# Four edits to a two-layer graph kernel: a sort moved by some products, banks of another pool, products with the identity, and joins a step later

## The chip, the cores and the metric

The kernel runs on one NeuronCore of a Trainium2 chip. The core has a matrix engine (TensorE, PE in the profile; PEld is its weight load), VectorE (DVE), ScalarE (ACT), GpSimd (POOL), and queues that start transfers (SP is SyncE's). Each engine works through its own instructions in their order and waits for others by semaphores. Matrix products go to PSUM, which has eight banks; a bank holds 128 rows of 512 float32 numbers.

The metric is the device time of one launch in microseconds (us). All times below are us unless they are marked otherwise.

## What is computed

`x` is 2708 x 1024 and `adj` 2708 x 2708, nearly all zeros and ones by a random draw whose density falls with the product of the row's and the column's weight: some rows have many neighbours, most only a few. Two layers follow each other, each with a residual and a layer norm:

```python
q, k, v = x @ W_q.T + b_q, x @ W_k.T + b_k, x @ W_v.T + b_v
z = scale * (q @ k.T) * adj
attn = softmax(where(z == 0, -10000, z), axis=1)
x = layernorm(x + relu(attn @ v))            # layer 0
x = layernorm(x + adj @ (x @ weight) + bias) # layer 1
```

## The kernel before

The kernel does not form the full score matrix. It lists each row's neighbours, gathers their rows of `x`, and does softmax and weighted sum over those alone. A second, dense way (`dense_part`) stands behind a flag and isn't taken for these inputs.

Rows are worked in 22 blocks of 128, after a sort by degree: block 0 holds the rows of highest degree, and the rows of the very highest ("the hub") are shared out over all partitions. `SLOTS` says how many neighbours a row of each block may have.

The stages, in the order of time:

1. *Weights and M.* W_q and W_k are transposed, and M = W_q^T W_k is formed in 28 steps (`product_of_m`), each of four matmuls of 128 x 128 by 128 x 512 into one bank; the profile shows two records for each float32 matmul, so 8 records a step. The steps follow Strassen's scheme with seven half products per pair of blocks. The partial sums of four accumulators `pa` are added to M by VectorE or copied by ScalarE (L322, L806) between the steps that reuse the same bank. Meanwhile VectorE lists the neighbours of the blocks of `adj` (`list_columns`: six FIND_INDEX8 at L237 and some small work for each block) and ScalarE counts them (`count_columns`, L253, 2.5 each). A block of `adj` lies in one of three buffers; when it is counted, `load_adj` issues the next load on SyncE's queue. `EARLY` blocks are listed during M, in even steps of its 28 products; the rest during the next stage.
2. *Four pairs of y blocks* (`y_pair`, blocks 0 to 7): y = x M by seven half products of 8 records per pair. VectorE adds three of the results (L322, yo), the others are copied by ScalarE; a pair's seventh product accumulates into a bank that one of these additions has to read first. `between` hangs pieces of other work behind the half products of this stage, by their running number (`began`): behind the first, third and fifth product of a pair a count, behind the second and fourth a list.
3. *Fourteen single y blocks* (`y_block`, and `y_last` for the rest of 20 rows), two banks of eight matmuls each; ScalarE copies the banks (L320). Beside them runs the attention of the high-degree blocks: GpSimd gathers rows (L464, L480), VectorE forms scores (L1016) and weighted sums (L1073, L1150), ScalarE exponentials (L1052, L1143). Which blocks are worked on beside which step follows from a planner with costs and a credit (`run_job`, `credit`).
4. *Ten pairs of blocks of layer 0* (`project_pair`), with their transposes (`flip`, L935), and one step for rows without neighbours ("mean").
5. *Layer 1*: ten units of two blocks, whose neighbours' normed rows are gathered from DRAM and summed (`sum_rows`, L1446, L1449), transposed and multiplied with the weight.

The sort has two halves, called families (blocks 0 to 7, and the rest). `sort_begin` makes class numbers from the degrees and one-hot rows `hot` on VectorE (L654 to L669), as soon as the family's blocks are listed and counted; `sort_end` multiplies them with a triangle and with ones on TensorE (L675, L679), turns the result into positions on VectorE (L683 to L690) and builds records. `records_out` scatters the records to DRAM by GpSimd (L704), eight instructions for the first family, then reads the tables back (L714 to L720). `deal_hub` is a generator whose parts are taken one at a time: it gathers the hub's records (L464, `rec_r`) and computes from them where the hub's rows lie (L533, `hub_i`).

In the version before, the first family's `sort_end` is called within M, after product 26, and its records go out behind the start of the first y pair's second product.

The hub and block 0 end with two "joins", in which the partitions that share a row agree on the maximum (transpose at L1158, VectorE at L1160 to L1165) and on the sum (matmul at L1168, VectorE at L1170 to L1173). `join(i, least)` runs a join at step `i` if the last part of this block was at least `least` steps ago.

PSUM is split into a pool of four banks for products (`bank()`, tile `po`), three banks for transposes (`spare_bank()` and tile `tr`) and one for small results (`mm`). Each pool hands its banks out in turn, and whoever is given a bank waits until its last reader is done.

The program is written in Python; the order of the instructions on each engine is made from it by the tile framework, which moves an instruction ahead of others that aren't ready by its own estimate. Additions and copies out of PSUM in `add` have high priority (`URGENT`). `follow(later, earlier)` adds a dependency by hand; with `same=True` it only fixes the order on one engine.

Of the kernel before, what the change touches and what calls it, by code (L numbers as in the profile page):

```python
# [27 lines left out]
HUB_SLOTS = 11  # L28
HUB_KEYS = 80
RUN = 12  # L30
FAMILY = 8


# [4 lines left out]
KEYS = 24  # L38
RANGES = 6
CLASSES = list(range(1, 14)) + [15, 17, 20, 24]  # L40
EARLY = 12
G1 = 9
RB = 5
REC = 28
# [38 lines left out]
def sparse_part(ctx, tc, x, xT, adj, wqT, wkT, wvT, bq, bk, bv, w1, b1, out):  # L83
# [28 lines left out]
    with es:  # L112
# [198 lines left out]
        def bank():  # L311
            return p_o.tile([P, HALF], F32, name="po")

        def spare_bank():
            return p_tr.tile([P, 4, P], F32, name="tr").rearrange("p a b -> p (a b)")
# [57 lines left out]
        def y_block(b):  # L373
            yo = yos[b % 3]
            to = halves_of(yo)
            firsts = []
            for h in range(NH):
                po = bank()
                for c in range(DC):
                    put = nc.tensor.matmul(po, xts[b][:, c, :], m_q[c // 4][h][:, c % 4], start=(c == 0), stop=(c == DC - 1))  # L380
                    if c % (DC // 2) == 0:
                        firsts.append(put)
                add(to[h], po, None)
            products.append(put)
            if b != NB - 2:
                column_sums(b, firsts)
            if b == NB - 4:
                column_sums(NB - 2, [put] * (DC // 2))
            load_x()
            y_store(b, yo)  # L390
# [280 lines left out]
        def sort_end(f, behind=None):  # L671
            b0, nb = families[f]
            bs, NKB = slice(b0, b0 + nb), NK * nb
            before = spare_bank() if f else p_mm.tile([P, HALF], F32, name="mm")
            put = nc.tensor.matmul(before[:, :NKB], lower, hot_f[f], start=True, stop=True)  # L675
            if behind is not None:
                follow(put, behind, same=True)
            total = spare_bank()
            nc.tensor.matmul(total[:, :NKB], ones, hot_f[f], start=True, stop=True)  # L679
            one_row = lists.tile([P, NKB], F32, name=f"one_row{f}")  # L680
            nc.vector.memset(one_row, 1.0)
            upto = lists.tile([P, NKB], F32, name=f"upto{f}")
            nc.vector.tensor_tensor_scan(upto, one_row, total[:, :NKB], 0.0, op0=ALU.mult, op1=ALU.add)  # L683
            nc.vector.tensor_sub(upto, upto, total[:, :NKB])
            nc.vector.tensor_add(upto, upto, before[:, :NKB])
            nc.vector.tensor_mul(upto, upto, hot_f[f])
            pos = lists.tile([P, nb], F32, name=f"pos{f}")
            nc.vector.tensor_reduce(pos, by_class(upto, nb).rearrange("p k b -> p b k"), AX.X, ALU.add)
            pos_i = (xa if f else lists).tile([P, nb], I32, name=f"pos_i{f}", bufs=1)
            nc.vector.tensor_copy(pos_i, pos)  # L690

            rec = (xa if f else lists).tile([P, nb, REC], I32, name=f"rec{f}", bufs=1)
            nc.vector.memset(rec[:, :, ROW:], 0)
            fill = lists.tile([P, nb, ROW], F32, name=f"fill{f}")
            nc.vector.tensor_scalar(fill, keys[:, bs, :], 0.0, float(N + 1), op0=ALU.is_equal, op1=ALU.mult)
            nc.vector.scalar_tensor_tensor(rec[:, :, 0:ROW], keys[:, bs, :], -1.0, fill, op0=ALU.add, op1=ALU.add)
            nc.vector.tensor_copy(rec[:, :, ROW], own[:, bs])
            nc.vector.tensor_copy(rec[:, :, DEG], deg[:, bs])
            nc.vector.tensor_scalar_add(rec[:, :, OFF], own[:, bs], float(-b0 * P))
            return f, nb, rec, pos_i  # L700
# [49 lines left out]
        def product_of_m(acc, a, w, start, stop):  # L750
            nonlocal done, worked
            put = half_products(acc, a, w, start, stop)
            worked += 1
            if counted[0] < done:
                count_columns(put)
            while done < EARLY * worked // (7 * DC // 2):
                list_columns()
                done += 1
                if done == FAMILY + 1:
                    sort_begin(0)  # L760
            if not sorted_ and done > FAMILY + 2 and worked > 7 * DC // 2 - 4:
                sorted_.append(sort_end(0, put))

        half = range(DC // 2)
        (w11, w12), (w21, w22) = wk_o
# [82 lines left out]
            count_columns(began[-1])  # L848
        for b in range(0, FAMILY, 2):
            first = len(began)  # L850
            for k in range(min(4 if b == 2 else 3, NB - done)):
                if k:
                    between[first + 2 * k] = [lambda put: list_columns()]
                else:
                    list_columns()
                done += 1
                between[first + 2 * k + 1] = [count_columns]
            if b == 4:
                between[first + 6] = [lambda put: next(deal)]
            if b == 6:  # L860
                between[first + 5] = [lambda put: next(deal)]
            y_pair(b)
            if b == 0:
                records_out(*sorted_[0], 0, FAMILY, began[first + 1])
                records_back(0)
            if b == 2:
                load_last()
                bcast_rows(y_bc, y_col)
            if b == 4:
                sort_begin(1)  # L870
            if b in (0, 6):
                next(deal)
            if b >= 4:
                load_wv(range(DC // 2 + b - 4, DC // 2 + b - 2))
# [469 lines left out]
        for i, (kind, b) in enumerate(steps):  # L1344
# [3 lines left out]
            pending = []  # L1348
            credit += COST.get(kind, COST.get(b, STEP - Y_END))
            step[0] = i  # L1350
            join(i, 2 if left_y else 1)
            if kind == "y" and b == NB - 3:
                (q11, q12), (q21, q22) = wv_q
                follow(nc.vector.tensor_sub(q12, q12, q11), products[-2])
# [124 lines left out]
        def work1(unit, A, S, xrs):  # L1479

            ts = [wa.tile([P, D], F32, name="t", tag="t" if k % 2 == 0 else "yg") for k, _ in enumerate(unit)]
            sums = [[stat.tile([P, 1], F32, name=f"sm{h}", bufs=6) for h in range(NH)] for _ in unit]

            def whole(k, h, acc, what):
                with tc.high_priority(URGENT):
                    nc.vector.scalar_tensor_tensor(halves_of(ts[k])[h], acc, 1.0, what, op0=ALU.mult, op1=ALU.add,  # L1486
                                                   accum_out=sums[k][h])
                    if k and unit == units[-1]:
                        if len(sums[k]) == NH:
                            sums[k].append(half_stats())  # L1490
                        nc.vector.bn_stats(out=sums[k][-1][:, h, :], in_=halves_of(ts[k])[h])

            xs_ = [halves_of(xr) for xr in xrs]
            pair_products(A, S, w1_q, w1_t, xs_, xs_, whole, unit == units[-1])
            return ts, sums

        got1, turned1, pending = {}, {}, []
        got1[0] = [sum_rows(b, k) for k, b in enumerate(units[0])]
# [349 lines left out]
```

## Time and profile before

| | |
|---|---|
| median of five runs | 1090.85 |
| lowest and highest of the runs | 1086.36 and 1091.83 |
| the profiled execution's own time | 1079.33 |
| its span | 1077.6 |
| busy: PE, DVE, POOL, ACT | 960.5, 839.8, 542.9, 411.0 |
| mean granted TensorE clock | 0.96 |

The stages as they stand in the profile, with what the windows of 20 us give for TensorE and VectorE:

| stage | about | PE busy of 20 | DVE busy of 20 |
|---|---|---|---|
| M's products | 28 to 137 | 20 up to 100, then 15.8 and 13.0 | 19.8 to 20.0 |
| pairs of y | 137 to 248 | 13.9 to 20 | 12.8 to 20 |
| single y blocks | 250 to 465 | 18 to 20 up to 340, then 10.1 to 19.7 | 7 to 18.5 |
| pairs of layer 0 | 472 to 769 | 14.9 to 20 | 13.4 to 20 |
| layer 1 | 777 to 1078 | 16.5 to 20 | 5.7 to 18.9 |

All profile numbers come from one execution, recorded by the hardware. In a timeline a line begins with the start and the duration in us, then engine, line of the kernel, operation, output and inputs, shape and the number of records; in brackets stands how long the engine was idle before and what ended that. In a list of waits the numbers are the total, how often, and the longest.

### The profile page before, as it was taken

How to read it: one execution, taken by the hardware profiler on the slowest of the kernel's cores; microseconds unless marked ns; L12 is line 12 of the kernel's file. 1: busy time of each engine (PE TensorE's matmuls, PEld its weight loads, DVE VectorE, ACT ScalarE, POOL GpSimd, SP SyncE). 2: the span in 40 equal slices, each digit the busy share in tenths (PEclk: the TensorE clock that was granted, in tenths of full speed). 3: DMA queues.
4: the chain of work that ended last, by engine and by line, in shares of the span. 5: the costliest groups of instructions: out<-in, count | busy, mean ns of one | idle time of the engine just before them, and what ended most of it. 6: DMA issues, size and time to landing. Idle time of an engine off the chain costs nothing.

```text
span 1077.6 us, 10401 instructions
## 1 busy us (share of the span) xinstructions
PE 960.5 (89%) x2697; PEld 451.0 (42%) x2697; DVE 839.8 (78%) x2033; ACT 411.0 (38%) x917; POOL 542.9 (50%) x447
## 2 busy tenths in 40 slices
PE   7999598999999796778999979999499999989894
PEld 6444233444444342334454434443154444445341
DVE  7999997974667777975999979777469878779532
ACT  4353175544532232422544444331312443351621
POOL 0431343122755655461767653346388877778510
PEclk9999799899999898889999999999789999999998
DMA  8565587388887665473558876479698789997731
GB/s 347 185 193 169 168 262 244 121 279 199 225 254 248 211 192 171 128 219 85 159 152 252 224 206 194 168 245 303 220 247 282 235 258 308 323 263 208 207 112 42
DMA packets 103069, 229.23 MB, mean 213 GB/s; under 512 B 19678, under 2 KB 47078, under 8 KB 103000
## 3 DMA queue, kind: packets, MB, share of 16 engines
q0 software_dynamic: 51152, 159.06, 49.1%
q1 hardware_dynamic: 51848, 69.41, 19.9%
q8 instruction: 23, 0.38, 0.1%
q14 instruction: 46, 0.38, 0.1%
HBM read 218.10 MB, written 33.64 MB: 234 GB/s over the span
## 4 chain that ended last, share of the span: by engine, by line
issue 17%; PE 15%; DMA 13%; DVE 12%; POOL 11%; ACT 1%; POOLq 0%; DVEq 0%; ACTq 0%
PE po L300 13%; POOL g L480 4%; DMA g<-in_x_dram,tabs 4%; DVE junkv L1016 3%; DMA g<-x_d,tabs 2%; POOL xr L464 2%; DMA xr<-x_d,tabs 2%; DVE r L1073 2%; DVE r L1449 1%; POOL g L464 1%; DMA yg<-y_d,tabs 1%; POOL tab_d L704 1%; DVE t L322 1%; DMA g<-in_x_dram,tab_h 1%; DMA g<-in_x_dram,tab 1%
## 5 line engine op out<-in xcount | busy, mean ns | idle before, releaser
L380 PE MATMUL po<-m,xt 128*128 128x512 f32 x416 | 187.1, 610 | 18.3 <-ACT yo L320 18.3
L300 PE MATMUL po<-t,s_all 128*128 128x512 f32 x320 | 148.3, 607 | 16.0 <-DVE t L322 8.0
L480 POOL DMA_INDIRECT g<-in_x_dram,tabs x84 | 113.3, 1349 | 87.2 <-issue 16.1
L380 PEld LDWEIGHTS po<-m,xt 128*128 128x128 f32 x416 | 80.9, 196 | 122.0 <-issue 98.8
L1016 DVE SCALAR_TENSOR_TENSOR junkv<-yg,g 128x1024 uint8<-128x1024 f32 x69 | 84.3, 1221 | 35.0 <-DMA g<-in_x_dram,tabs 24.3
L1449 DVE SCALAR_TENSOR_TENSOR r<-g,valid,r 128x1024 f32<-128x1024 f32 x77 | 98.3, 1282 | 12.9 <-DMA g<-x_d,tabs 12.5
L300 PEld LDWEIGHTS po<-t,s_all 128*128 128x128 f32 x320 | 61.1, 194 | 98.4 <-issue 70.8
L480 POOL DMA_INDIRECT g<-x_d,tabs x66 | 75.8, 1149 | 22.4 <-issue 15.9
L978 ACT ACTIVATE junks<-t,lnm 128x1024 uint8<-128x1024 f32 (+1 forms) x40 | 45.9, 1148 | 102.3 <-DVE lnm L976 99.8
L1073 DVE SCALAR_TENSOR_TENSOR r<-g,pr,r 128x1024 f32<-128x1024 f32 x64 | 81.8, 1280 | 4.0 <-ACT r L1071 3.7
L237 DVE FIND_INDEX8 at_a<-ones,a 128x8 uint16<-128x83 f32 (+3 forms) x132 | 82.8, 632 | 0.0
L300 PE MATMUL po<-wv,s_all 128*128 128x512 f32 x160 | 74.0, 606 | 7.4 <-DVE t L322 5.8
L253 ACT ACTIVATE junk<-a 128x2756 uint8<-128x2756 uint32 (+1 forms) x22 | 55.1, 2503 | 59.3 <-issue 22.1
L300 PE MATMUL po<-w,rT 128*128 128x512 f32 x160 | 73.8, 602 | 1.7 <-DVE t L1486 1.6
L300 PE MATMUL po<-t,rT 128*128 128x512 f32 x160 | 72.6, 595 | 1.7 <-DVE t L322 1.1
L300 PE MATMUL po<-wv,rT 128*128 128x512 f32 x160 | 72.7, 606 | 0.0
L300 PE MATMUL po<-w,s_all 128*128 128x512 f32 x160 | 72.3, 592 | 0.0
L936 ACT COPY rT<-tr 128x512 f32<-128x512 f32 x76 | 41.4, 586 | 74.7 <-PE tr L935 69.8
L991 ACT ACTIVATE t<-t,nmr,rstd 128x1024 f32<-128x1024 f32 (+1 forms) x40 | 49.1, 1240 | 53.4 <-DVE nmr L990 44.7
L453 ACT ACTIVATE junka<-xt 128x128 f32<-128x128 f32 x168 | 51.9, 309 | 36.5 <-PE po L300 25.9
L1016 DVE SCALAR_TENSOR_TENSOR junkv<-xr,g 128x1024 uint8<-128x1024 f32 x37 | 45.2, 1222 | 24.5 <-DMA g<-in_x_dram,tabs 11.2
L935 PE MATMUL tr<-ident,r 128*128 128x128 f32 x304 | 40.7, 283 | 23.4 <-DVE r L1446 14.3
(410 smaller groups left out, 1705.1 us busy)
## 6 DMA issues: line engine op xcount, KB each, us to landing
xt<-in_xT_dram SPq DMA_DIRECT2D x21, 512.0 KB
y_d<-yo SPq DMA_DIRECT2D x21, 512.0 KB
a<-in_adj_dram SPq DMA_DIRECT2D x21, 413.5 KB
a<-in_adj_dram SPq DMA_DIRECT2D x21, 338.5 KB
a<-in_adj_dram SPq DMA_DIRECT2D x21, 263.5 KB
wq_i<-in_wqT_dram SPq DMA_DIRECT2D x8, 512.0 KB
wk_i<-in_wkT_dram SPq DMA_DIRECT2D x8, 512.0 KB
wv<-in_wvT_dram SPq DMA_DIRECT2D x16, 256.0 KB
```

Of the source, the lines that this page charges most:

```text
L237: nc.vector.max_index(at[:n, i], ones[:n, :8], a[:n, cuts[i] + 8 * i:cuts[i + 1] + 8 * i + 8])
L253: put = nc.scalar.activation(junk[:n], loaded[b][:n, :AW].bitcast(U32), AF.Sign, accum_out=cnt[:n, b:b + 1])
L300: put = nc.tensor.matmul(acc, a[:, k], w[:, k], start=start and k == 0, stop=stop and k == DC // 2 - 1, skip_group_check=True)
L380: put = nc.tensor.matmul(po, xts[b][:, c, :], m_q[c // 4][h][:, c % 4], start=(c == 0), stop=(c == DC - 1))
L453: put = nc.scalar.activation(junka[:, :xt.shape[2]], xt[:, c, :], AF.Copy, accum_out=xs[:, c, b:b + 1])
L480: nc.gpsimd.indirect_dma_start(out=dst[:n], out_offset=None, in_=src, in_offset=bass.IndirectOffsetOnAxis(ap=at, axis=0), bounds_check=N - ...
L936: nc.scalar.copy(rT[:, g * 4:g * 4 + 4, :], tr)
L978: nc.scalar.activation(junks[:n], t[:n], AF.Square, bias=nm[:n], accum_out=vs[:n])
L991: applied.append(nc.scalar.activation(t[:n], t[:n], AF.Identity, bias=nmr[:n], scale=rstd[:n]))
L1016: nc.vector.scalar_tensor_tensor(junkv[:n], yg[:n], scale, xg[:n], op0=ALU.mult, op1=ALU.mult, accum_out=s)
L1073: nc.vector.scalar_tensor_tensor(r[:n], xg[j][:n], pr[:n, j:j + 1], r[:n], op0=ALU.mult, op1=ALU.add)
L1449: put = nc.vector.scalar_tensor_tensor(r[:n], xg[:n], ok[:n, j:j + 1], r[:n], op0=ALU.mult, op1=ALU.add)
```

## The change

Four edits are made at once:

- `EARLY` goes from 12 to 13, so one more block is listed during M, and the second y pair lists three blocks instead of four. The first family's `sort_end` is no longer called in `product_of_m`; it hangs behind the third half product of the first y pair, and the records go out behind the start of the fourth instead of the second.
- In `y_block`, blocks with a remainder of 1 by 3 (10, 13, 16 and 19) take their two banks from the transposes' pool instead of the products' pool.
- While y blocks are left, a join runs three steps after the last part of its block, not two.
- Between the layers TensorE gets 13 matmuls of the identity with half of `y_bc` (128 x 512, float32) into one bank of the transposes' pool. Nothing reads the result. They stand behind layer 0's last product in TensorE's order.

```diff
+WARM = 13
-EARLY = 12
+EARLY = 13
@@ y_block
-                po = bank()
+                po = spare_bank() if b % 3 == 1 else bank()
@@ product_of_m
-            if not sorted_ and done > FAMILY + 2 and worked > 7 * DC // 2 - 4:
-                sorted_.append(sort_end(0, put))
@@ the y pairs
-            for k in range(min(4 if b == 2 else 3, NB - done)):
+            for k in range(min(3, NB - done)):
...
+            if b == 0:
+                between[first + 3] = [lambda put: sorted_.append(sort_end(0, put))] + between.get(first + 3, [])
...
             if b == 0:
-                records_out(*sorted_[0], 0, FAMILY, began[first + 1])
+                records_out(*sorted_[0], 0, FAMILY, began[first + 3])
                 records_back(0)
@@ the steps of layer 0
-            join(i, 2 if left_y else 1)
+            join(i, 3 if left_y else 1)
@@ before layer 1's first sums
+        warm = spare_bank()
+        for k in range(WARM):
+            put = nc.tensor.matmul(warm, ident, y_bc[:, :HALF], start=True, stop=True, skip_group_check=True)
+            follow(put, products[-1], same=True)
```

## The prediction

> **What bounds the kernel now.** I read the table of windows first (which stage leaves which engine idle), then the waits of TensorE, then the timelines of the engines around each edit, then the chain that ended last.
>
> TensorE's waits, longest first: four of these rows are what the change aims at (ACT yo, DVE r L1446, DVE hot, DVE den).
>
> ```profile
> PE po L380 <- ACT yo L320: 18.3, 5, 9.9
> PE tr L935 <- DVE r L1446: 14.3, 1, 14.3
> PE mm L675 <- DVE hot L669: 11.2, 1, 11.2
> PE po L300 <- DVE yo L322: 10.3, 3, 6.1
> PE mm L1168 <- DVE den L1164: 5.0, 1, 5.0
> ```
>
> The first sort, TensorE's timeline: products 25 and 26 of M end at 115.8, the sort's matmul waits for its one-hot rows, products 27 and 28 follow in 8.94 where 16 such records take 7.03 elsewhere, and later two seventh products of y pairs wait for an addition.
>
> ```profile
> 108.78 7.03 PE L300 MATMUL po<-wk_o,wq_o 128*128 128x512 f32 x16
> 127.00 0.87 PE L675 MATMUL mm<-hot,lower 128*128 128x152 f32 x2 [11.19 <-DVE hot L669]
> 128.18 8.94 PE L300 MATMUL po<-wk_o,wq_o 128*128 128x512 f32 x16
> 136.96 7.03 PE L300 MATMUL po<-m,xt 128*128 128x512 f32 x16
> ...
> 160.32 3.70 PE L300 MATMUL po<-y_t,xt 128*128 128x512 f32 x8 [2.60 <-DVE yo L322]
> ...
> 190.77 6.72 PE L300 MATMUL po<-y_t,xt 128*128 128x512 f32 x8 [6.15 <-DVE yo L322]
> ```
>
> VectorE's side of it: from 40 to 160 the windows give it 19.8 to 20.0 busy of every 20, so it is the bound there and TensorE's waits are its symptoms. It adds M's last partial sum 14.7 after product 24 ended (108.8), and its only idle time before 190 is 7.20 for the hub's record.
>
> ```profile
> 123.47 0.68 DVE L322 TENSOR_TENSOR m<-po,m 128x512 f32<-128x512 f32 x1
> 159.59 0.68 DVE L322 TENSOR_TENSOR yo<-po,yo 128x512 f32<-128x512 f32 x1
> 167.46 0.21 DVE L533 TENSOR_SCALAR hub_i<-rec_r,g_col 128x1 int32<-128x1 int32 x1 [7.20 <-DMA rec_r<-tab_d,r_i]
> ```
>
> The single y blocks' end, ScalarE's timeline: the last two copies stand behind a softmax exponential that waits for VectorE, and the first transposes of layer 0's pairs are copied after them.
>
> ```profile
> 466.69 0.59 ACT L320 COPY yo<-po 128x512 f32<-128x512 f32 x1
> ...
> 469.94 0.29 ACT L1052 ACTIVATE pr<-scores,nms 128x2 f32<-128x2 f32 x1 [2.36 <-DVE nms L1043]
> ...
> 470.23 1.05 ACT L320 COPY yo<-po 128x512 f32<-128x512 f32 x2
> 471.18 1.57 ACT L936 COPY rT<-tr 128x512 f32<-128x512 f32 x3
> ```
>
> The change of layers: TensorE stands 14.31 and starts slow (8 transposes 1.94, later 1.04).
>
> ```profile
> 764.97 3.60 PE L300 MATMUL po<-t,rT 128*128 128x512 f32 x8
> 782.87 1.94 PE L935 MATMUL tr<-ident,r 128*128 128x128 f32 x8 [14.31 <-DVE r L1446]
> 784.63 2.07 PE L300 MATMUL po<-w,rT 128*128 128x512 f32 x2
> ```
>
> **Part 1, the first sort.** Removed: the wait of 11.19 in TensorE's queue. Moved: two matmuls (127.00 to 128.18, 1.2) behind the third product of the first y pair, VectorE's chain on them (133.05 to 135.27, 2.2), GpSimd's eight scatters of records (141.71 to 154.04) and, after them in its queue, the table reads and the hub's gather. Added to M's stage: one list of a block (4.70, the distance of the starts 77.10, 81.80, 86.50), taken from the second y pair (4 to 3). The counts behind the products come one or two products sooner, and with them their loads in SyncE's queue. These share it with the x tiles (issued at 107.58, landed at 116.08); the first sums of x are done at 126.0 and needed by the third y product, so some 5 us of delay there cost nothing.
>
> What is late next: product 28 accumulates into the bank that the addition at 123.47 reads, so without the sort TensorE still waits, from 119.2 (product 27 at 3.4) to 124.15. The first y product would start at 127.6 instead of 136.96, 9.4 earlier. By product 24 eleven lists are asked for instead of ten, so the addition moves by up to 4.7, and the gain shrinks to 4.7. Then the seventh y product: its addition ended at 160.27 with VectorE never idle since 40. With one list more ahead of it, it ends at 165.0, with none at 160.3; halfway, since the pair's own four lists fill that stretch either way: 162.6, so here TensorE is 2.3 later in spite of the wait removed. Then the hub's record. The scatters now follow the fourth product instead of the second. The sort's matmuls end at 132.3 + 10.3 + 1.2 = 143.8, VectorE's lag on them was 4.7 (128.4 to 133.05) and its chain 2.2, so the scatters start at 150.7 instead of 141.7, and the record lands at 176.5. If the instruction that needs it moves back in VectorE's order by as much, which two lists fill, the 7.20 vanish; the seventh product of the second pair is then limited by VectorE at 190.7 - 7.2 + 2.3 = 185.8 and by TensorE at 162.6 + 3.7 + 20.6 (163.86 to 184.5) + 1.9 for a slow start = 188.8. I take 188.8: 2 earlier, and a warm 3.6 instead of 6.72, together -5. From there every pair and the attention's first gathers (of stored y, at 255.57) follow TensorE, so it goes through. Ends: VectorE's limit without any more list, 183.5 (190.7 - 7.2), with the 3.1 of clock and the third pair's wait of 1.5: -12; and +8, worked out as the first rival. The value lies nearest to the limit by TensorE's own rows.
>
> **Part 2, banks of single y blocks, and the hub's joins.** Four blocks (10, 13, 16, 19) use two of the three transposes' banks; every block then needs the copy of three blocks ago instead of two, 13.8 us of room. The waits of 18.3 and, by the joins a step later, of 5.0 should go. But from 340 to 470 TensorE isn't on the chain: it goes through gathers, scores and sums (VectorE 13 to 18.5 of 20), and ScalarE's copies stand in its queue behind their exponentials. Block 20 ended at 464.9 and was copied at 470.23; were it done 20 earlier, the copy would still be behind the exponential at 469.94, and so the last store of y (471.31), the gather after it (478.98) and the transposes' copies. I cost both at 0: what hides them is that queue. If its order changes so that these copies come ahead of 465.62 (where ScalarE waits 4.40) they land up to 10 earlier: -10. Against it: block 19's banks are freed by the copy at 466.69, and the flips that started at 464.75 need them: +1.5 (three take 1.47). The bound stays near 0 as long as the copies stand where this row has them. [...]
>
> **Part 3, thirteen unit products.** One costs 0.86 (8 records, four products, every 3.43). 13 x 0.86 = 11.2 in an idle 14.31; 3.1 are left. The cold start costs 0.90 + 1.05 + 0.43 = 2.4 (8 transposes 1.94 against 1.04, 2 records 2.07 against 1.02, 8 transposes 1.47 against 1.04). Will 3.1 idle keep it warm? After 2.60 idle (160.32) 8 records took 3.70, after 3.06 (756.30) 5.40: so it may be cold again. And GpSimd issues gathers from 777.30 on with 0.30 between them, VectorE waits 1.14 for one at 824.57 and TensorE for VectorE at 834.99: most of what is won is gone by then. -1; ends -2.4 and +1.
>
> [...]
>
> **Sum:** -5 + 0 - 1 = -6 on the profiled execution's own 1079.33 us (span 1077.6): 1073.3. It lies 11.5 below the median of the runs (1090.85), so I carry the difference: 1085.
>
> **Rivals.** *The record comes too late (slower).* VectorE reaches the hub's instruction at 165.0 with one list more, in an unchanged order, and waits until 176.5: 11.5 instead of 7.20. The second pair's seventh product then comes at 190.7 + 9.0 (record) - 4.7 (list taken away) = 195, +4.3; the first pair's wait grows from 2.6 to 7 or more and costs a cold start on its path, some 3: +8 in all, 1099. It decides once VectorE's wait for the record exceeds 7.2 + 4.7 = 11.9 from its old place. For it: VectorE has no slack; against it: lists are there to fill the time. *The y pairs get all that VectorE allows:* -12, 1078. For it: additions are urgent in the order; against it: one list more. *ScalarE's order changes too:* -10 with the forecast's, 1075. Against it: nothing in part 2 makes the softmax earlier. *Nothing arrives:* part 1 at 0, 1090.
>
> **How the numbers follow.** Forecast 0.35 (own range 1081 to 1089), late record 0.25, VectorE's limit 0.12, ScalarE's order 0.12, nothing 0.16. A measurement of this kernel tells about 0.3% (3.3 us) from no change. Faster: 0.24 of the two early cases and 0.32 of the forecast, 0.56; same 0.19; slower 0.25. The range leaves out half of the tails beyond 1070 (both early cases together reach below it) and 1099.
>
> **What would show it.** Right: no wait on hot; a wait on m<-po's addition of about 5 to 10 before product 28; the seventh products of the first two pairs at about 163 and 189 from the span's start; hardly any wait of L380 but still copies at the attention's pace, ending some 5 before 470; 13 products behind 764, and nothing left of them at 835. Wrong: a wait at L533 above 12; last copies ahead of the last exponential; attention that starts later than 264.

## The result and the profile after

Over 44 runs the changed kernel took 1085.76 us in the median (1077.07 to 1094.01). 86 runs of the kernel before, on the same chips, took 1086.75 (1078.24 to 1095.54). The ratio is 0.999, with a 95% interval of 0.9977 to 1.0004: between 2.5 faster and 0.4 slower, and so no change that can be told. The forecast of 1085 lies beside it by luck, not by its own sum: it took 6 away from a median of five runs (1090.85) that was 4 too high.

The profiled executions differ by more than the kernels do: 1079.33 before, near the lower end of its runs, and 1086.25 after, about its median. What follows compares places within them, and lengths of stages, not their ends. Line numbers are one higher in every kernel that holds the unit products, L301 for L300.

TensorE's waits in the profile after, in the same view as before (total, how often, longest). The wait on the one-hot rows is gone, the five waits for copies of y (18.3) have become one of 25.0, ahead of the block of the last 20 rows, the wait for the first transposes' copies has grown from 5.6 to 17.2, and the 14.3 between the layers are 3.1:

```profile
PE po L432 <- ACT yo L321: 25.0, 1, 25.0
PE tr L936 <- ACT rT L937: 18.2, 2, 17.2
PE po L301 <- issue: 13.2, 3, 12.2
...
PE po L301 <- DVE yo L323: 7.7, 1, 7.7
...
PE tr L936 <- DVE r L1447: 3.1, 1, 3.1
...
PE po L301 <- DVE m L323: 2.1, 1, 2.1
```

The first sort, TensorE's timeline after. The first y product starts at 126.33 instead of 136.96. But the first pair's seventh product starts at 159.82 (160.32 before) after 12.22 idle, and the second pair's at 194.70 (190.77 before):

```profile
117.66 8.83 PE L301 MATMUL po<-wk_o,wq_o 128*128 128x512 f32 x16 [2.12 <-DVE m L323]
126.33 7.03 PE L301 MATMUL po<-m,xt 128*128 128x512 f32 x16
...
136.62 0.42 PE L676 MATMUL mm<-hot,lower 128*128 128x152 f32 x2
...
159.82 6.61 PE L301 MATMUL po<-y_t,xt 128*128 128x512 f32 x8 [12.22 <-issue]
...
194.70 6.24 PE L301 MATMUL po<-y_t,xt 128*128 128x512 f32 x8 [7.66 <-DVE yo L323]
```

VectorE after. It now reaches the hub's instruction at 166.46 (174.37 less 7.91 idle; 160.26 before) and waits as long as before, since the record lands 6.9 later. Soon after, two tiny instructions (128 x 15 numbers) take 2.58 and 1.23; the first took 0.15 in the kernel before:

```profile
174.37 0.21 DVE L534 TENSOR_SCALAR hub_i<-rec_r,g_col 128x1 int32<-128x1 int32 x1 [7.91 <-DMA rec_r<-tab_d,r_i]
...
178.94 2.58 DVE L728 TENSOR_TENSOR valid<-places,deg 128x15 f32<-128x15 f32 x1
...
181.62 1.23 DVE L729 TENSOR_SCALAR less<-valid 128x15 f32<-128x15 f32 x1
```

They lie under GpSimd's four sums of x for a later pair:

```profile
177.74 1.29 POOL L396 TENSOR_TENSOR y_s<-xt 128x512 f32<-128x512 f32 x1
178.97 1.28 POOL L399 TENSOR_TENSOR y_s<-xt 128x512 f32<-128x512 f32 x1
180.20 1.28 POOL L397 TENSOR_TENSOR y_s<-y_s,xt 128x512 f32<-128x512 f32 x1
181.56 1.27 POOL L398 TENSOR_TENSOR y_s<-xt,y_s 128x512 f32<-128x512 f32 x1
```

The end of the single y blocks, ScalarE after. The last two copies of y come at 465.50 instead of 470.23. The transposes' copies, which came right behind them, now stand behind an exponential of block 0's last piece, for which ScalarE is idle 12.97:

```profile
465.50 1.07 ACT L321 COPY yo<-po 128x512 f32<-128x512 f32 x2
479.54 0.29 ACT L1141 ACTIVATE turn<-nm 128x1 f32<-128x1 f32 x1 [12.97 <-DVE nm L1138]
...
480.02 1.53 ACT L937 COPY rT<-tr 128x512 f32<-128x512 f32 x3
```

TensorE there and at the change of layers: layer 0's first pair starts at 481.55 (472.73 before). The thirteen products fill 11.32; the eight transposes behind them are quick (1.06 at a granted clock of 1.00, instead of 1.94 at 0.50), but the four products' records after them take 3.58, at 0.53, where four cost 1.88 at 1.00 (797.96):

```profile
480.64 1.12 PE L936 MATMUL tr<-ident,r 128*128 128x128 f32 x4 [17.23 <-ACT rT L937]
481.55 9.53 PE L301 MATMUL po<-wv,rT 128*128 128x512 f32 x16
...
774.35 11.32 PE L1500 MATMUL tr<-y_bc,ident 128*128 128x512 f32 x26
788.82 1.06 PE L936 MATMUL tr<-ident,r 128*128 128x128 f32 x8 [3.14 <-DVE r L1447]
790.12 3.58 PE L301 MATMUL po<-w,rT 128*128 128x512 f32 x4 [0.24 <-issue]
```

### The profile page after: what moved, and what is told of

Read it like the earlier page. It is cut to its first block, busy times and chain, and to the rows that moved or that the text cites. A ratio compares the mean times of both kernels' runs of the same rounds, so it can differ in the third digit from the quotient of the medians.

```text
span 1084.5 us, 10477 instructions
## 1 busy us (share of the span) xinstructions
PE 969.6 (89%) x2723; PEld 456.2 (42%) x2723; DVE 836.8 (77%) x2033; ACT 412.3 (38%) x917; POOL 551.5 (51%) x447
## 3 DMA queue, kind: packets, MB, share of 16 engines
q1 hardware_dynamic: 51848, 69.41, 19.9%
## 4 chain that ended last, share of the span: by engine, by line
PE 20%; issue 15%; DMA 14%; DVE 9%; POOL 9%; ACT 1%; POOLq 0%; DVEq 0%; ACTq 0%
PE po L301 17%; DMA g<-in_x_dram,tabs 5%; POOL g L481 4%; DVE junkv L1017 3%; DMA xr<-x_d,tabs 2%; DMA g<-x_d,tabs 2%; DVE r L1074 2%; POOL g L465 1%; DMA yg<-y_d,tabs 1%; POOL xr L465 1%; PE tr L936 1%; DMA g<-x_d,tab_h 1%; DVE r L1450 1%; DMA g<-in_x_dram,tab_h 1%; DVE t L323 1%
## 5 line engine op out<-in xcount | busy, mean ns | idle before, releaser
L301 PE MATMUL po<-t,s_all 128*128 128x512 f32 x320 | 146.8, 602 | 13.5 <-DVE t L323 8.3
L381 PE MATMUL po<-m,xt 128*128 128x512 f32 x288 | 124.8, 592 | 0.0
L301 PEld LDWEIGHTS po<-t,s_all 128*128 128x128 f32 x320 | 60.4, 192 | 95.5 <-issue 72.0
L481 POOL DMA_INDIRECT g<-x_d,tabs x66 | 78.3, 1186 | 23.2 <-issue 15.8
L381 PEld LDWEIGHTS po<-m,xt 128*128 128x128 f32 x288 | 54.5, 190 | 68.0 <-issue 67.0
L301 PE MATMUL po<-w,rT 128*128 128x512 f32 x160 | 75.3, 612 | 4.4 <-DVE t L1487 4.2
L301 PE MATMUL po<-wv,s_all 128*128 128x512 f32 x160 | 73.9, 606 | 4.8 <-DVE nms L1044 2.5
L301 PE MATMUL po<-t,rT 128*128 128x512 f32 x160 | 73.7, 603 | 1.5 <-DVE t L323 1.0
L301 PE MATMUL po<-w,s_all 128*128 128x512 f32 x160 | 73.2, 598 | 0.0
L301 PE MATMUL po<-wv,rT 128*128 128x512 f32 x160 | 73.2, 609 | 0.0
```

Of the source, the lines that this page charges most:

```text
L301: put = nc.tensor.matmul(acc, a[:, k], w[:, k], start=start and k == 0, stop=stop and k == DC // 2 - 1, skip_group_check=True)
L481: nc.gpsimd.indirect_dma_start(out=dst[:n], out_offset=None, in_=src, in_offset=bass.IndirectOffsetOnAxis(ap=at, axis=0), bounds_check=N - ...
```

## The experiments

Each median is of 12 runs, and each ratio is against runs of the kernel before on the same chip, with its 95% interval; 0.001 is 1.09 us. "Later record" is one more edit that some of them have:

```diff
@@ after a y pair
-            if b in (0, 6):
+            if b in (2, 6):
                 next(deal)
```

With it the hub's record is asked for, and used, one y pair later.

| kernel | median | ratio | interval |
|---|---|---|---|
| part 1 alone | 1088.39 | 1.0017 | 0.9985 to 1.0050 |
| banks alone | 1088.38 | 1.0038 | 1.0011 to 1.0066 |
| joins alone | 1084.92 | 0.9997 | 0.9965 to 1.0030 |
| banks and joins (part 2) | 1084.08 | 0.9996 | 0.9963 to 1.0029 |
| 13 unit products alone (part 3) | 1084.81 | 0.9975 | 0.9938 to 1.0013 |
| 26 unit products alone | 1087.38 | 1.0007 | 0.9976 to 1.0038 |
| the change, 12 lists in M's stage | 1083.35 | 0.9952 | 0.9922 to 0.9982 |
| the change, later record | 1082.69 | 0.9953 | 0.9922 to 0.9984 |
| the same without the later joins | 1089.22 | 1.0015 | 0.9986 to 1.0043 |
| later record alone | 1080.18 | 0.9940 | 0.9909 to 0.9970 |
| later record, banks, unit products | 1084.22 | 0.9994 | 0.9961 to 1.0027 |
| later record, banks, unit products, joins | 1076.85 | 0.9920 | 0.9887 to 0.9952 |

The stages of the profiled executions: the end of the y pairs; from there to the first product of layer 0's pairs; from there to the start of the last product of layer 0; from layer 1's first transposes to the end. They are read from TensorE's timeline and the end of the span.

| kernel | y pairs end | to layer 0 | layer 0's pairs | layer 1 |
|---|---|---|---|---|
| before | 248.4 | 224.3 | 292.2 | 294.7 |
| the change | 250.1 | 231.4 | 289.4 | 295.7 |
| part 1 alone | 249.4 | 228.4 | 295.9 | 301.5 |
| banks alone | 249.2 | 230.9 | 288.2 | 298.2 |
| joins alone | 248.0 | 228.8 | 292.4 | 304.3 |
| banks and joins | 249.1 | 229.4 | 290.9 | 298.0 |
| 13 unit products | 247.9 | 227.5 | 292.1 | 297.9 |
| 26 unit products | 250.2 | 225.5 | 290.7 | 293.3 |
| the change, 12 lists | 249.3 | 229.3 | 286.0 | 299.6 |
| the change, later record | 246.9 | 229.6 | 287.5 | 299.1 |
| the same without later joins | 250.3 | 231.0 | 296.4 | 296.0 |
| later record alone | 245.8 | 225.3 | 293.9 | 294.6 |
| later record, banks, units | 240.7 | 230.1 | 292.8 | 300.6 |
| the same with joins | 240.4 | 229.3 | 286.2 | 300.2 |

Layer 1, which only the unit products touch, spreads from 293.3 to 304.3. A stage of one profile is therefore not read to a few us. Groups of profiles are.

### Part 1 alone

```diff
-EARLY = 12
+EARLY = 13
@@ product_of_m
-            if not sorted_ and done > FAMILY + 2 and worked > 7 * DC // 2 - 4:
-                sorted_.append(sort_end(0, put))
@@ the y pairs
-            for k in range(min(4 if b == 2 else 3, NB - done)):
+            for k in range(min(3, NB - done)):
...
+            if b == 0:
+                between[first + 3] = [lambda put: sorted_.append(sort_end(0, put))] + between.get(first + 3, [])
...
-                records_out(*sorted_[0], 0, FAMILY, began[first + 1])
+                records_out(*sorted_[0], 0, FAMILY, began[first + 3])
```

> Part 1 alone (first sort behind the third half product of the first y pair, one list more in M's stage) on the kernel before. Theory (VectorE and the late record eat the gain): TensorE's wait of 11.19 on the one-hot rows goes and the first y product starts about 10 earlier, but the first pair's seventh product stays at 160 (within 2), since VectorE works without a pause up to it; VectorE's wait for the hub's record stays between 6 and 10 (7.20 before), the record lands near 174 instead of 167.5, and the second pair's seventh product comes at 193 to 196 instead of 190.8. The y pairs end 1 to 3 later than in the kernel before; time -0.1% to +0.3% against the kernel before. Rival, the forecast on record: the wait for the record vanishes, the second pair's seventh product is at 189 or earlier, and the time is 5 lower (-0.5%). Rival, the late record as I priced it: +8 (+0.7%).

Measured: 1.0017, from 1.6 faster to 5.4 slower. The forecast's -5 lies outside, the rival's +8 too. The first y product starts at 124.60, the first pair's seventh at 159.40, the record's wait is 7.66 and ends at 173.68, the second pair's seventh starts at 193.74, and the y pairs end at 249.4, 1.0 later than before. The theory holds at each of these places: of the 12.4 won at 125, 0.9 are left at 159, and at 194 it is 3.0 behind.

### The change with twelve lists in M's stage

```diff
-EARLY = 13
+EARLY = 12
@@ the y pairs
-            for k in range(min(3, NB - done)):
+            for k in range(min(4 if b == 2 else 3, NB - done)):
```

> The changed kernel with twelve blocks listed in M's stage again and four in the second y pair; the sort stays behind the third half product of the first pair. Theory (VectorE, never idle up to the first pair's seventh product, sets it, and a list costs it 4.7): the seventh product of the first pair comes at 154 to 157 instead of 159.8, the record lands 2 to 5 earlier than 174.4, and the second pair's seventh product, with its list back, at 191 to 195; y pairs end at 247 to 250, and the time is that of the changed kernel within 0.3%. Rival (TensorE or the copies set the first pair's seventh product, the list lies beside them): it stays within 1 of 159.8, and the second pair's comes 4 later than 194.7.

The theory's place was missed: with a list less ahead of it, the first pair's seventh product starts at 159.90, as the rival said, though VectorE has no idle time up to there. The record lands at 174.08, only 0.3 earlier, and the second pair's seventh product comes at 192.29, in the theory's range and not 4 later. The reason stands in VectorE's groups. Counted by the first search of each list, 17 lists are begun before this addition in the changed kernel and in part 1 alone, 16 in the kernel before and in this one. What a list more costs, the small instructions of the sort give back. These are VectorE's groups between 100 and 160 (busy us, mean ns), first of the kernel before:

```profile
L666 DVE SCALAR_TENSOR_TENSOR kk<-deg,kk 128x8 f32<-128x8 f32 x17 | 5.2, 303 | 0.0
L669 DVE TENSOR_SCALAR hot<-kk 128x8 f32<-128x8 f32 x19 | 5.0, 341 | 0.0
L667 DVE TENSOR_TENSOR kk<-past,kk 128x8 f32<-128x8 f32 x1 | 1.2, 1219 | 0.0
```

then of the changed kernel:

```profile
L667 DVE SCALAR_TENSOR_TENSOR kk<-deg,kk 128x8 f32<-128x8 f32 x17 | 2.6, 155 | 0.2
...
L670 DVE TENSOR_SCALAR hot<-kk 128x8 f32<-128x8 f32 x19 | 1.6, 168 | 0.0
...
L668 DVE TENSOR_TENSOR kk<-past,kk 128x8 f32<-128x8 f32 x1 | 0.2, 160 | 0.0
```

The same work costs 11.4 before and 4.4 after. In the kernel before it meets GpSimd's sums of x (116.08 to 125.97); in the changed kernel it is done by 114.7, and those sums start at 119.42. In the kernel with twelve lists the one-hot rows cost 5.0 again, since they meet the sums from 115.67 on. Of the 7.0 won the changed kernel loses some to other instructions that meet the sums later (one of 2.28 takes 3.35 at 140.00). So the order of two engines, not the wait on hot alone, decided what part 1 could give here.

The time is 0.9952, lower than the changed kernel's 0.999. In this profile the y pairs end only 0.8 earlier; where the rest of the 4 us comes from, this run doesn't show.

### The later record: in the changed kernel, and alone

> The changed kernel with one thing altered: the hub's record is asked for after the second y pair instead of after the first, so that VectorE meets the instruction that needs it about 25 later. Theory (late record): VectorE's wait of 7.91 for the record vanishes or falls below 1, the second pair's seventh product comes at 186 to 190 instead of 194.7, the y pairs end 4 to 8 earlier than in the changed kernel, and the time is 3 to 7 below the changed kernel (-0.3 to -0.6%), unless the hub's own gathers then come too late for the first attention steps: in that case the wait comes back behind the y pairs, at the hub's scores, and the time is equal or higher. Rival (VectorE's saturation alone is the limit): the seventh product stays within 1 of 194.7 and the time is equal to the changed kernel's.

> The kernel before with the hub's record asked for after the second y pair instead of after the first, and nothing else. Theory (the wait for the record is a cost of VectorE by itself, and the sort's move only made room for nothing): VectorE's wait of 7.20 at the hub's record is gone, the second pair's seventh product comes at 184 to 188 instead of 190.8, the y pairs end 3 to 6 earlier than 248.4, and the time is 3 to 6 below before (-0.3 to -0.5%): as much as the whole change with the same alteration, which measured 0.9953 of before. Rival (the record's wait matters only where the sort is moved): seventh product within 1 of 190.8 and the same time as before.

Alone on the kernel before: 0.994 (3.3 to 9.9 faster), the largest effect of any single edit. VectorE's wait for the record falls from 7.20 to 2.5, with 2.4 at a table that is read back earlier in its order, and the second pair's seventh product starts at 185.67 instead of 190.77. In this profile the third pair's seventh product then runs slowly (6.53), and the y pairs end only 2.6 earlier. VectorE's waits between 160 and 200 in this kernel:

```profile
DVE hub_i L533 <- DMA rec_r<-tab_d,r_i: 2.5, 1, 2.5
DVE deg L737 <- DMA tab<-tab_d: 2.4, 1, 2.4
```

In the changed kernel: 0.9953. I had expected the wait to vanish there, and it did not. It went to the next instruction that needs what the late scatters wrote:

```profile
DVE degs L741 <- DMA tabs<-tab_d: 7.1, 1, 7.1
DVE deg L738 <- DMA tab<-tab_d: 2.0, 1, 2.0
...
```

So with the sort moved, the records themselves are too late, whoever asks first. The ends of the y pairs in the table agree. With the sort where it was, they are 247.9 to 250.2 in six profiles, and 240.4, 240.7 and 245.8 with the later record. With the sort moved, they are 249.3 to 250.1 in three, and 246.9 and 250.3 with it. That the seventh product still came at 191.38 instead of 194.70 has another cause, which the next kernel shows.

### The later record without the later joins

```diff
-            join(i, 3 if left_y else 1)
+            join(i, 2 if left_y else 1)
```

> The changed kernel with the record asked for a pair later and with the joins two steps after, as they were. Theory (the joins' turn in ScalarE's order costs what it gives back in the pairs): the wait for the first transposes' copies falls from 17.3 to below 6, the first product of layer 0's pairs starts 3 to 6 earlier than 476.5 in the kernel with later joins, the pairs take 3 longer, and the time is the same as that kernel's within 0.2% (0.993 to 0.998 of before). Rival (the turn costs the whole 8 that the start of the pairs shows): -0.4% or more beyond that kernel, 0.992 of before or less.

Neither was right: it is 0.6% slower than its neighbour, not equal and not faster. Two things differ in the profiles. One has nothing to do with the joins: up to 250 VectorE has the same instructions in the same order, yet the second pair's seventh product starts at 195.06 here and at 191.38 there. One instruction of VectorE makes it. In this kernel:

```profile
181.98 4.47 DVE L582 TENSOR_TENSOR deg_r<-deg_r,full 128x1 f32<-128x1 f32 x1
```

and in its neighbour:

```profile
182.04 0.15 DVE L582 TENSOR_TENSOR deg_r<-deg_r,full 128x1 f32<-128x1 f32 x1
```

GpSimd's sums start at 182.69 here and at 182.75 there. An instruction on one number per partition was through at once in one kernel, and in the other lasted until the third of these sums, of 1.28 each, was done. It starts 0.71 ahead of the first sum in both, so what decided between the two, the traces don't show. The other difference is the joins' own: layer 0's pairs took 296.4 against 287.5, and the wait for the transposes' copies fell to 10.9, not below 6. It is taken up with the next four kernels.

### Banks and joins

```diff
@@ y_block: the banks
-                po = bank()
+                po = spare_bank() if b % 3 == 1 else bank()
@@ the steps of layer 0: the joins
-            join(i, 2 if left_y else 1)
+            join(i, 3 if left_y else 1)
```

Both together:

> Part 2 alone (four single y blocks in the transposes' banks, joins three steps after) on the kernel before. Theory (ScalarE's order): the last copies of y come some 4 to 5 earlier than 470.2, but the copies of the first transposes of layer 0's pairs now stand behind block 0's last maximum, in ScalarE's order; TensorE waits for them about 17 instead of 5.6, and the first pair's product of layer 0 starts 7 to 9 later than in the kernel before (472.7). If later stages follow TensorE all the way, the time is 7 to 9 higher (+0.7 to +0.8%); if they follow GpSimd's gathers for the pairs, which start earlier, it is within 3 of before. Rival, the pricing on record: 0 (+-0.2%), with the start of layer 0's pairs where it was. Rival: the removed waits of 18.3 and 5.0 arrive, -5 to -10.

The joins alone:

> The joins three steps after, alone, on the kernel before. Theory: this edit alone turns ScalarE's order round: the first transposes of layer 0's pairs are copied behind block 0's last maximum, and TensorE waits 16 to 19 for them instead of 5.6; TensorE's waits for the copies of y stay near 18 in total, since no bank is added; the first product of layer 0's pairs starts 475 to 480 after the span's start; then 3 come back in the pairs. Time 0 to +0.3% against before. Rival (the order is turned by the banks): waits and starts as before, within 2.

The banks alone:

> The banks of four single y blocks alone, joins two steps after, on the kernel before. Theory (without the later joins the banks cost: TensorE runs ahead, but the last copy of y and the first transposes' copies still stand behind the hub's softmax in ScalarE's order): TensorE's waits of 18.3 for the copies of y in the single blocks are gone up to the last block, the last copies come 465 to 479 after the span's start, the first product of layer 0's pairs starts 229 to 232 after the end of the y pairs instead of 224.3, the pairs take 291 to 296, and the time is 3 to 6 above before (1.003 to 1.005). Rival (the pricing on record: worth 0): 224 to 228 after the end of the y pairs and 0.998 to 1.002. Rival (the waits arrive): 0.996 or less.

Both together measured 0.9996 and do to ScalarE's order what the whole change does: the wait for the transposes' copies is 17.39 and layer 0 starts 229.4 after the y pairs (at 478.49, 5.8 later than before, not 7 to 9). The joins alone turn this order round too, though the wait is 11.93 (5.61 before) and not 16 to 19. They leave the waits for copies of y at 19.9 and the time at 0.9997, and layer 0's pairs are no shorter (292.4). The banks alone are slower: 1.0038 (1.2 to 7.2 slower). With them TensorE's waits for copies of y are indeed gone up to the block of the last 20 rows, where it then stands 23.2 in one piece. The last copy comes later, not earlier (478.11 against 470.23). ScalarE with the banks alone:

```profile
465.08 0.58 ACT L320 COPY yo<-po 128x512 f32<-128x512 f32 x1
475.35 1.05 ACT L475 COPY yg<-y_bc 128x1024 f32<-128x1024 f32 x1 [9.68 <-DVE junkv L1016]
477.81 0.30 ACT L1052 ACTIVATE pr<-scores,nms 128x2 f32<-128x2 f32 x1 [1.42 <-DVE nms L1043]
...
478.11 0.57 ACT L320 COPY yo<-po 128x512 f32<-128x512 f32 x1
478.57 1.56 ACT L936 COPY rT<-tr 128x512 f32<-128x512 f32 x3
```

One copy has gone ahead of the exponential at L1052, the other still stands behind it, and the exponential is 8 later than the 469.94 of before. It is not the hub's, as the expectation has it: the hub's and block 0's are at L1143, and L1052 belongs to the other blocks, here one with two slots. So the banks have a price, and it lies in the stage from the y pairs to layer 0: 224.3, 228.4, 227.5, 225.5 and 225.3 without either edit, mean 226.2; 230.9, 231.0 and 230.1 with the banks alone, mean 230.7; 229.3 to 231.4 with both. The price stays when the joins come later, but layer 0's pairs become shorter: 286.0 to 290.9 in the five profiles with both, mean 288.0, against 292.8 in the mean of the eight without later joins (288.2 to 296.4; the 288.2 is that of the banks alone, where 291 to 296 was said). In the kernel before, the first of these pairs has a wait of 2.71 at 491.35. All eight profiles without the later joins have it (2.26 to 3.52), none of the six with them does, the joins alone included. Where the rest of the 4.8 comes from isn't shown.

The pairing of the two edits was tried once more, on top of the later record:

> The kernel before with the record asked for a pair later, with the banks and with the unit products, and without the sort's move and without the later joins. Theory (the record's wait is the only part with a gain of its own; banks and unit products are worth nothing): 0.994 of before, as with the later record alone, within 0.3%. Rival (the waits that the banks remove arrive when the joins stay): 0.990 or less. Rival (the kernel with all four edits but the later joins measured 1.0015 with the later record, so banks without later joins cost some 6): 0.999 or more.

> The same with the joins three steps after. Theory (the later joins turn ScalarE's order, which costs some 5 at the start of layer 0's pairs and gives back as much in them): the same as its neighbour without later joins, within 0.3%, the first transposes' copies waited for by 15 to 19 instead of 5 to 11. Rival (later joins gain 0.6%, as the difference of the two kernels with the moved sort and the later record would have it, 0.9953 against 1.0015): 0.988 or less, and the gain would have to show behind 475, in the pairs of layer 0 or in layer 1.

Without the later joins 0.9994, with them 0.9920. The rival was right in the first: banks without later joins take back what the later record gives. In the second it was right in the gain, not in its 0.988, which it counted from 0.994. The later joins bring 0.7% here, 0.6% in the neighbouring pair above (1.0015 to 0.9953) and 0.4% on the kernel before (1.0038 to 0.9996), where the intervals overlap; in two of these three comparisons it is seen in layer 0's pairs (292.8 to 286.2 and 296.4 to 287.5), in the third not (288.2 to 290.9). On their own they bring nothing that can be told. This last kernel, later record and parts 2 and 3 without part 1, is faster than both kernels of this study: 1076.85 in the median, 5.2 to 12.3 below before.

### Unit products

```diff
+WARM = 13
...
+        warm = spare_bank()
+        for k in range(WARM):
+            put = nc.tensor.matmul(warm, ident, y_bc[:, :HALF], start=True, stop=True, skip_group_check=True)
+            follow(put, products[-1], same=True)
```

> Part 3 alone (thirteen unit products between the layers) on the kernel before. Theory: they fill 11.2 of the 14.3 idle, about 3.1 stay idle, the first eight transposes take 1.06 instead of 1.94, but the products after them run at the slow clock (eight records at 5.4 or four at 3.6, instead of 3.6 and 1.05), so that the time is within 1 of before (-0.1% to +0.1%). Rival: the clock stays up, the stage is 2.4 earlier and GpSimd doesn't take it back: -0.2%. Rival: the unit products end later than the first sums and push them back: +0.1% or more; then no idle time would be left ahead of the first transposes of layer 1.

The same with `WARM = 26`:

> Twenty-six unit products instead of thirteen between the layers, alone, on the kernel before. They take 26 x 0.86 = 22.4, some 8 more than the 14.3 idle, so that layer 1's first transposes start 8 late. If TensorE's start of layer 1 is on the path to the end: +5 to +7 (+0.5%), since 2 come back by the warm clock. If layer 1 is paced by the gathers and sums, which go on meanwhile: the delay is made up within the first units, TensorE then has no wait for the sums of rows until about 820, and the time is that of before within 0.2%. The second would mean that part 3 could bring nothing whatever the clock did.

Thirteen alone: 0.9975, an interval with zero in it, and a middle below the bound that I had put on it. The clock behaved as expected, slow again in the first products (3.55 for four records; the granted clock from 785 to 790 is 0.66). Twenty-six reach far beyond the idle time, and the first 24 records of transposes then follow without a pause:

```profile
769.83 22.48 PE L1500 MATMUL tr<-y_bc,ident 128*128 128x512 f32 x52
792.14 2.91 PE L936 MATMUL tr<-ident,r 128*128 128x128 f32 x24
```

TensorE starts layer 1 at 25.8 behind layer 0's last product instead of 17.9, 7.9 later, and the kernel measures 1.0007, at most 4.1 slower. The +5 to +7 of a start that counts in full are excluded; 3 or 4 are not. Layer 1 took 293.3 in this profile, the shortest of all. But TensorE's later waits on sums did not disappear as I had said (3.7 on one of them), so the picture of a stage paced by gathers alone isn't shown either.

## Why the prediction was right and wrong

**The sum.** -6 was forecast, -1.0 came, with -2.5 as the most that the interval allows. The three parts alone add up to +1.9 - 0.4 - 2.7 = -1.2, near it, though each of them is known only to 3 or 4. The time of 1085.76 is within the stated range of 1081 to 1089 because the base was 4 too high, not because the parts behaved as said: from 1086.75 the same sum gives 1080.8.

**Part 1 is the step that failed: -5 was said, +1.9 came (-1.6 to +5.4).** The steps up to the first y product were right, even too careful: no wait on hot, a wait for an addition to M, though ahead of product 27 and not 28, and 2.12 instead of 5 to 10, and y starts at 126.33 instead of 127.6 to 132.3. The first pair's seventh product was said to come at 162.6 and came at 159.82: VectorE was the bound, as said, but the sum held only the list more and not what the sort's own small instructions cost under GpSimd's sums (11.4 against 4.4). What decided was the sentence that the 7.20 for the record vanish if the instruction moves back in VectorE's order. It moved back by 6.2 and the record by 6.9, so the wait stayed: 7.91. That the record landed near what was said (174.37, said 176.5) is luck. The sort's matmuls ended at 137.30, earlier than the 143.8 of the sum, but VectorE's chain came 14.1 behind them and not 4.7, so the scatters began at 155.78 and not at 150.7; but from the end of the last scatter to the hub's gather 3.6 passed, not the 11.1 of before, since two of the table reads now came behind it. The second pair's seventh product came at 194.70, not at 188.8, and not warm (6.24, at a granted clock of 0.59).

**The rival of the late record is what happened there.** It said that VectorE arrives at 165.0 and the product starts at 195; measured 166.46 and 194.70. Counted from the instruction's old place (160.26), the record came 14.1 later, beyond its bound of 11.9. Its price was wrong in what follows: +8 was said, and at the end of the y pairs +1.7 is left. The first pair's seventh product was no later than before, but ran slowly, as the rival said (6.61 at a granted clock of 0.55, instead of 3.70 at 1.00). The second pair's was 3.9 later. The third then needs 27.55 after the second's seventh product instead of 29.70, as its wait of 1.51 is gone. That attention would start later than 264 was named as a sign against the forecast: its first score from y comes at 265.86 instead of 264.18.

**Part 2: 0 was said and -0.4 came, by the wrong reason.** The copies were not hidden in an unchanged queue. The queue's order changed, the end named as -10 came in half (copies 4.7 earlier) and brought nothing at its place, since the transposes' copies fell behind another exponential: 8.8 later, beyond the +1.5 that was the bound. The condition was written down ("as long as the copies stand where this row has them"), the chance that they move was put at 0.12, and it covered the gain only. The 0 is the sum of two effects, the banks at +0.4% and, on top of them, the later joins at -0.4%, of which the sum had neither.

**Part 3: -1 was said, -2.7 came (-6.7 to +1.4).** Of the two rows that the estimate weighed, the one of 3.06 idle (eight records in 5.40, at a granted clock of 0.68) came nearer than the one of 2.60 (3.70, at 1.00): after 3.14 idle four records took 3.58, at 0.53. But 3.06 is no bound either: 2.31 idle at 762.25 in the changed kernel was followed by eight records of 5.40 (0.68), and 2.71 at 491.35 in the kernel before by eight of 3.70 (1.00). Whether a gain is there can't be told.

## What to carry to other kernels

Moving a step later also moves everything that it feeds: compare when the consumer comes and when its data lands, both after the move. A wait shrinks only if the consumer moves by more than the data, and goes only if it moves by the whole wait more. Ask what a removed wait was hiding on the engine behind it, here small VectorE instructions under GpSimd's sums, before adding work in its place. And a 0 that rests on the order of a queue is two unknown numbers, since the order made by the tile framework can change with a small edit, as it did here with the joins alone; test such edits apart, and take the base from as many runs as the effect needs.

## What the runs showed of the hardware

VectorE and GpSimd held each other up in these runs. Instructions of VectorE on 128 x 15 or fewer numbers that take 0.13 to 0.17 elsewhere took 0.67 to 1.22 in the sort of the kernel before (L666 and L667, 116.70 to 121.11), 2.58 in the changed kernel (L728) and 4.47 in the one with the later record and without the later joins (L582), beside GpSimd's additions of 128 x 512. GpSimd's additions took 3.20 to 3.32 instead of 1.27 beside VectorE's of 128 x 2048 (the changed kernel, 121.87, 137.90 and 141.28). Under GpSimd's sums in the changed kernel, VectorE's search over 128 x 685 (0.88 at 120.66, 0.86 to 0.87 elsewhere) and its addition out of PSUM (0.69 at 120.00, 0.67 to 0.69 elsewhere) were not lengthened by more than 0.02. The ends lie together: VectorE's instructions of 0.67 to 1.22, 2.58 and 4.47 ended 0.02 to 0.04 after one of GpSimd's additions had ended, the one of 4.47 after the third of three, and GpSimd's three long additions ended 1.13 after VectorE's of 128 x 2048. The one of 4.47 had started 0.71 ahead of the first of the three sums, so starting first did not get it through. The same instruction in the same order, equally far ahead of the sums, took 0.15 in the neighbouring kernel, and what decides isn't shown.

The clock behind the unit products did not follow from the idle time. After 2.81, 2.84, 3.13 and twice 3.14 idle the next four records of products took 3.34 to 3.58; after 2.80 and 2.86 idle they took 1.98. The granted clock was 1.00 in the first eight transposes behind the gap in the changed kernel (788.8 to 790.0), then 0.59 (790 to 792); with the later record it stayed at 1.00 (780 to 790). These are TensorE's lines in the kernel with the unit products alone:

```profile
785.12 1.06 PE L936 MATMUL tr<-ident,r 128*128 128x128 f32 x8 [2.81 <-DVE r L1447]
786.42 3.55 PE L301 MATMUL po<-w,rT 128*128 128x512 f32 x4 [0.24 <-ACT rT L937]
```

and in the changed kernel with the later record:

```profile
781.58 1.06 PE L936 MATMUL tr<-ident,r 128*128 128x128 f32 x8 [2.86 <-DVE r L1447]
782.88 1.98 PE L301 MATMUL po<-w,rT 128*128 128x512 f32 x4 [0.24 <-ACT rT L937]
```

A gap of 2.81 was thus followed by slow products and one of 2.86 by quick ones. What decides between them, the traces don't show.
